# Sorting neighbour lists on the VectorE: exchanges and products in operations of at most 384 elements

## The chip, the cores and the metric

The kernel runs on one core of a Trainium2 chip. The core has five engines that work side by side, each with its own queue of instructions: PE (matmuls), DVE (elementwise work on vectors), ACT (activations and copies), POOL (GpSimd, which here issues the indirect DMAs), and SP (which issues the plain DMAs). The metric is the device time of one execution in microseconds. Several timed executions are made without the profiler, and one more with it; the profile is of that one.

## The reference

There are 16 graphs of 1024 nodes with 64 features each. Of every graph's adjacency matrix some edges are dropped by a rule on degrees. Then each node takes, for each feature, the quartiles of the values of its remaining neighbours, itself included, adds them with weights to its own value, and sends the sum through a two-layer perceptron.

```python
h = jnp.maximum(_layernorm(x, axis=-1), 0.0)
# inside the layer, with x = h:
adj_d = jnp.where(rem, 0.0, adj_)            # rem: the dropped edges, made symmetric
nd = adj_d > 0
vals = jnp.where(nd[..., None], x[:, None, :, :], jnp.inf)
s = jnp.sort(vals, axis=2)                   # the neighbours' values, sorted, per feature
nv = nd.sum(2)
for tau, w in zip((0.25, 0.5, 0.75), (0.25, 0.5, 0.25)):
    pos = tau * jnp.maximum(nv - 1, 0)
    lo, hi = jnp.floor(pos), jnp.ceil(pos)
    agg = agg + w * (v_lo + (pos - lo) * (v_hi - v_lo))   # v_lo, v_hi: s at lo and hi
out = x + agg
y = jax.nn.relu(out @ W1 + b1) @ W2 + b2
return x_in + y * mask
```

A node has few neighbours, so the kernel doesn't sort over 1024 values: it gathers the neighbours' rows and sorts short lists.

## The kernel before

Graphs ("batches" in the code) are prepared one by one: `load`, `drop`, `keep`, `order` and `collect` turn the adjacency matrix into lists of neighbour indices. `order` arranges the nodes of a graph by their number of neighbours, in eight tiles of 128 nodes: tile 0 has the longest lists, tile 7 the shortest. The tiles are put into four classes, by the number of slots that a list gets:

```python
CLASSES = (((0,), 13), ((1, 2, 3), 11), ((4, 5), 9), ((6, 7), 7))
```

Two graphs make a pair, and there are eight pairs. For each class of a pair there is one buffer `g` of shape [128 nodes, slots, tiles, 2 graphs, 64 features] in 32-bit floats. One slot of it, over all tiles of the class and both graphs, thus has 128 elements in a partition for tile 0, 384 for tiles 1 to 3, and 256 for tiles 4 and 5 and for tiles 6 and 7. The buffer is filled by indirect DMAs from POOL, one for each slot of each tile and graph (`gather`, line 1250): 128 rows of 256 bytes each. There are 1008 of them in all. The longest 32 lists of a graph are kept aside and sorted eight graphs at a time, in a group buffer `gg` of 24 slots with 128 elements each.

`sort` (line 1271) works on one buffer after the other. Its plan (`PLANS`) is a list of steps. A step takes `n` slots from place `a` with stride `da`, and `n` slots from `b` with stride `db`. With `f` at zero or more it is a full exchange: the minima (or maxima) of the two go to free slots from `f` on (line 1288), and the other of the two goes in place, over `a` or `b` (line 1289). With `f` below zero only one of the two is wanted (line 1285). After the steps the slots that hold the wanted ranks are multiplied by their weights (line 1296, the products, `taken` slots at a time), and 128x128 identity matmuls on PE add them up in PSUM (line 1298). The DVE does all steps and products; `n` is up to 3 for tile 0 and the group, up to 2 in the other classes, and the products of classes 9 and 7 take three slots at a time.

Two things go along with each step. The generator yields an estimated cost, and `weave` uses it to interleave the sort of one pair with the preparation of the next and with the issue of gathers. And `let_go` adds up these costs: from 0.8 on it puts a small memset of a tile `pause` (line 1268) behind the instruction that it is given.

The order in which the instructions were written is not the order in which the engines run them. `arrange` takes the whole program, works out which instruction depends on which, and plays it through with an estimated cost for each (for a DVE instruction (elements + 66) / 0.96 ns, and 115 ns more until a dependent one on the DVE can follow). Whenever an engine is free, it takes the earliest written instruction that is ready. The result is laid down as the fixed order of each engine. A `pause` stays tied to the instruction that it was put behind, and a run of matmuls (`settle`) is kept together.

Of the kernel before, what the change touches and what calls it, by code (L numbers as in the profile page):

```python
# [40 lines left out]
OP = mybir.AluOpType  # L41
# [4 lines left out]
C = 64  # L46
# [40 lines left out]
BIG = 3.0e38  # L87

SPREAD = 160


FIRST = CAPS[0] - 1
# [656 lines left out]
def list_layer(  # L749
# [14 lines left out]
    nc = tc.nc  # L764
# [10 lines left out]
    def settle(run):  # L775

        runs.append([ins.ins.name for ins in run])
        for ins, then in zip(run, run[1:]):
            tc.add_manual_dep(
                then.ins, ins.ins.name,  # L780
                mybir.DependencyInfo(mybir.DependencyClass.NoSync, mybir.DependencyReason.DATA),
                reason="order of a run",
            )
            tc.add_to_no_dep_group(f"run{len(runs)}", ins.ins)
            tc.info.no_tile_sem_insts.add(ins.ins.name)
        if len(run) > 1:
            tc.declare_fence(run[-1].ins, group=f"run{len(runs)}")
# [30 lines left out]
    plus, minus, upper, full, octet, one = (kw[:, lo:hi] for lo, hi in zip(FP8_PARTS, FP8_PARTS[1:]))  # L818
# [410 lines left out]
    def issue(many=None):  # L1229

        while queue and (many is None or many > 0):
            ins = queue.popleft()()
            if ins is None:
                continue
            turn[0] += 1
            many = None if many is None else many - 1
# [28 lines left out]
    def let_go(held, ins):  # L1265
        if held < 0.8:
            return held
        tails[nc.vector.memset(pause, 0.0).ins.name] = ins.ins.name  # L1268
        return 0.0

    def sort(lines, plan, first, coef, acc):

        size = lines.shape[2]
        held = 0.0

        def at(first, step, n):
            stop = first + step * (n - 1) + (1 if step >= 0 else -1)
            return lines[:, first:stop if stop >= 0 else None:step or 1]

        _, _, steps, ends, taken = plan  # L1280
        for n, a, da, b, db, f, df, back, what in steps:
            pa, pb = at(a, da, n), at(b, db, n)
            cost = 0.16 + n * size / 960
            if f < 0:
                ins = nc.vector.tensor_tensor(pa if back else pb, pa, pb, OP.min if what == "min" else OP.max)
            else:
                one, other = (OP.min, OP.max) if what == "<" else (OP.max, OP.min)
                nc.vector.tensor_tensor(at(f, df, n), pa, pb, one)  # L1288
                ins = nc.vector.tensor_tensor(pa if back else pb, pa, pb, other)  # L1289
                cost *= 2  # L1290
            yield cost
            held = let_go(held + cost, ins)
        for n in taken:
            now, ends = ends[:n], ends[n:]
            v = at(now[0], now[1] - now[0] if n > 1 else 0, n).rearrange("p s (k c) -> p s k c", c=C)
            ins = nc.vector.tensor_tensor(v, v, coef(first, n)[:, :, :, None].to_broadcast(list(v.shape)), OP.mult)
            settle([
                nc.tensor.matmul(  # L1298
                    acc, ident32, lines[:, s], start=False, stop=(s == now[-1] and not ends), skip_group_check=True
                )  # L1300
                for s in now
            ])
            first += n
            cost = 0.16 + n * size / 960
            held = let_go(held + cost, ins)
            yield cost
# [22 lines left out]
    def aggregate(m, o):  # L1329
# [4 lines left out]
        for half in (0, 1) if last else (1, 0):  # L1334
# [21 lines left out]
            for tiles, slots in parts:  # L1356
                lo, n = tiles[0], len(tiles)
                g = gathered.pop((m, tiles))
                plan = PLANS[slots]
                yield from sort(  # L1360
                    g.rearrange("p s n h c -> p s (n h c)"), plan, window(tiles, slots)[0],
                    lambda s, many: coef[:, s:s + many, lo:lo + n].rearrange("p s n h -> p s (n h)"),
                    acc[:, lo - 4 * half:lo - 4 * half + n],
                )
# [100 lines left out]
    def aggregate_group(grp):  # L1465
        n = GROUP // 4
        gg = groups.pop(grp)
        to, xg = gathered.pop(("group", grp))
        coef = wk.tile([P, TOP, n], F32, name="gcoef", bufs=1)
        weights(coef, group_num[grp][:, :, 1], n, TOP)  # L1470
        yield 1.0
        acc = psum.tile([P, n, C], F32, name="gacc", tag="agg", bufs=2)
        nc.tensor.matmul(acc, ident32, gg[:, CAP - 1], start=True, stop=False, skip_group_check=True)
        yield from sort(
            gg.rearrange("p s k c -> p s (k c)"), PLANS[CAP], window((0,), CAP)[0],
            lambda s, many: coef[:, s:s + many], acc.rearrange("p k c -> p (k c)"),
        )
        o = wk.tile([P, n * C], F32, name="go", tag="lows", bufs=1)
        nc.scalar.copy(o, acc.rearrange("p k c -> p (k c)"))
        yield 0.0  # L1480
        tp = psum.tile([P, P], F32, name="ot", tag="misc")
        nc.tensor.transpose(tp, o, ident32)
        ot = wk.tile([P, P], F32, name="got", tag="h1", bufs=1)
        nc.scalar.copy(ot, tp)
        yield 0.0
        h1 = wk.tile([P, n, P], F32, name="gh1", tag="highs", bufs=1)
        for k in range(n):
            hp = psum.tile([P, P], F32, name="hp", tag="misc")
            nc.tensor.matmul(hp, w1[k * C:(k + 1) * C], ot[k * C:(k + 1) * C], start=True, stop=True)
            nc.scalar.activation(h1[:, k], hp, AF.Relu, bias=b1c)  # L1490
            yield 0.0
        output(h1.rearrange("p k r -> p (k r)"), n, group_num.pop(grp)[:, :, 0], xg)
        gathered["out", grp] = to, xg
# [9 lines left out]
    def weave(main, total, side, side_total):  # L1503
# [3 lines left out]
        for cost in main:  # L1507
            done += cost / total
            issue(max(0, int(done * SPREAD) - turn[0]))
            while side is not None and spent / side_total < done:  # L1510
# [261 lines left out]
```

## Time and profile before

| what | us |
|---|---|
| timed runs, median of 3 (lowest to highest) | 2607.62 (2595.87 to 2612.22) |
| profiled execution, its own time | 1581.97 |
| span in the profile, first to last instruction | 1580.2 |
| POOL busy | 1137.8 |
| DVE busy | 1191.0 |
| PE busy | 1071.0 |
| ACT busy | 917.2 |
| gathers of line 1250, 1008 of them | 1089.7 |
| exchanges of lines 1288 and 1289, classes' buffers, 408 each | 280.7 and 281.4 |

The profile is of one execution. A line of the table of groups reads: line of the code, engine, operation, what is written and read, how many; then the busy time in us and the mean duration of one in ns; then the idle time of the engine just ahead of these instructions, and what ended it. A line of the waits reads: who waited, for what, us in total, number of times, the longest in us. A line of a timeline reads: start in us, duration in us, engine, line, operation, what is written and read. A line of the stretches reads: from and to in us, the length, and then the busy time of PE, PE's weight loads, DVE, ACT and POOL with their numbers of instructions.

### The profile page before, as it was taken

To read this page: it belongs to the slowest core of one execution; us is meant where nothing else is said; L and a number is where in the kernel's file an instruction comes from. 1 tells how busy PE (TensorE), PEld (TensorE's weight loads), DVE (VectorE), ACT (ScalarE), POOL (GpSimd) and SP (SyncE) were. 2 spreads that over 40 slices of the span, in tenths; PEclk is the share of its full clock that TensorE was granted. 3 is DMA by queue.
4 is the path that set the end of the run, shared out by engine and by line. 5 is a ranking of instruction groups with operands and counts; after the bars stand their busy time and mean duration, and the time that the engine had idled before them with its cause. 6 is when DMAs were issued, how large, how long until landed. Compare 5 with 4: busy or idle time off the path is not lost.

```text
span 1580.2 us, 25600 instructions
## 1 busy us (share of the span) xinstructions
PE 1071.0 (68%) x8385; PEld 664.2 (42%) x8385; DVE 1191.0 (75%) x3723; ACT 917.2 (58%) x2496; POOL 1137.8 (72%) x1051
## 2 busy tenths in 40 slices
PE   6777867889887887888569845588758822602235
PEld 3444544555554555455245534354535412301122
DVE  5615489865997789868884899977988897697660
ACT  6998886987958695978367841766825300200001
POOL 3277776777777777777777777777777777777730
PEclk9989979899998999899679976899888955855568
DMA  6453432442523252325122422222311211211100
GB/s 208 118 159 93 116 110 62 113 116 64 149 69 112 53 149 58 111 59 143 50 71 73 118 78 45 73 84 56 86 28 26 46 31 26 55 24 23 22 11 18
DMA packets 128481, 122.71 MB, mean 78 GB/s; under 512 B 94514, under 2 KB 95026, under 8 KB 128338
## 3 DMA queue, kind: packets, MB, share of 16 engines
q1 hardware_dynamic: 94994, 86.77, 19.4%
q0 software_dynamic: 33344, 34.21, 9.7%
q8 instruction: 68, 1.11, 0.3%
q14 instruction: 75, 0.61, 0.1%
HBM read 110.10 MB, written 9.07 MB: 75 GB/s over the span
## 4 chain that ended last, share of the span: by engine, by line
POOL 32%; ACT 20%; PE 14%; issue 14%; DVE 12%; DMA 6%; DVEq 0%; POOLq 0%; SPq 0%; ACTq 0%
POOL g L1250 31%; PE codeP L1072 5%; DMA g<-gtab,idx 4%; ACT dist L978 4%; ACT sg L891 3%; DVE g L1288 3%; ACT ne L911 3%; DVE g L1289 2%; ACT kept L1001 2%; ACT waste L1170 2%; ACT waste L1165 1%; ACT xt L1178 1%; PE acc L1298 1%; PE rk L968 1%; DMA xt<-in_x_dram 1%
## 5 line engine op out<-in xcount | busy, mean ns | idle before, releaser
L1250 POOL DMA_INDIRECT g<-gtab,idx x1008 | 1089.7, 1081 | 361.3 <-issue 288.0
L1288 DVE TENSOR_TENSOR g<-g 128x512 f32<-128x512 f32 (+3 forms) x408 | 280.7, 701 | 40.9 <-DMA g<-gtab,idx 25.9
L1289 DVE TENSOR_TENSOR g<-g 128x512 f32<-128x512 f32 (+3 forms) x408 | 281.4, 702 | 11.1 <-DMA gg<-g 8.4
L1298 PE MATMUL acc<-g,kf 128*128 128x256 f32 (+2 forms) x448 | 143.4, 461 | 176.5 <-DVE pause L1268 105.2
L1072 PE MATMUL codeP<-pack,perm 128*128 128x332 bf16 x1024 | 185.3, 323 | 21.4 <-DVE perm L1047 18.4
L978 ACT ACTIVATE dist<-rk,bias 128x512 f16<-128x512 f32 x256 | 168.4, 698 | 27.8 <-DVE bias L953 10.7
L1298 PEld LDWEIGHTS acc<-g,kf 128*128 128x128 f32 x448 | 89.5, 231 | 204.1 <-DVE pause L1268 111.4
L968 PE MATMUL rk<-kb,cnt 128*128 128x512 bf16 x256 | 113.2, 442 | 74.5 <-ACT dist L978 68.2
L1001 ACT ACTIVATE kept<-kp 128x512 fp8e4<-128x512 f32 x248 | 149.2, 617 | 14.0 <-PE kp L996 11.9
L898 PE MATMUL tp<-kb,sg 128*128 128x128 bf16 x1024 | 106.8, 243 | 69.3 <-ACT sg L891 52.6
L911 ACT ACTIVATE ne<-tp 128x512 fp8e4<-128x512 f32 x248 | 138.2, 608 | 19.4 <-PE tp L904 10.7
L973 PEld LDWEIGHTS <-ne 128*128 128x128 fp8e4 x1024 | 90.2, 109 | 133.1 <-issue 110.8
L1072 PEld LDWEIGHTS <-perm 128*128 128x128 bf16 x1024 | 93.9, 101 | 85.3 <-DVE perm L1047 43.9
L891 ACT ACTIVATE sg<-at 128x1024 bf16<-128x1024 f32 x121 | 126.6, 1076 | 2.4 <-DMA at<-in_adj_dram 2.3
L898 PEld LDWEIGHTS <-sg 128*128 128x128 bf16 x1024 | 81.2, 110 | 91.1 <-ACT sg L891 61.1
L973 PE MATMUL rk<-kw,ne 128*128 128x128 fp8e5 x1024 | 118.0, 243 | 0.0
L979 DVE TENSOR_SCALAR rem<-dist,half 128x1024 bf16<-128x1024 f16 x128 | 64.7, 506 | 61.7 <-ACT dist L978 60.7
L996 PE MATMUL kp<-kw,rem 128*128 128x128 fp8e5 x1024 | 99.7, 219 | 0.0
L991 PE MATMUL kp<-ne,kw 128*128 128x512 fp8e4 x256 | 98.5, 385 | 0.1
L992 PE MATMUL kp<-rem,kw 128*128 128x512 bf16 x256 | 97.6, 382 | 0.0
L1077 ACT CAST st<-codeP 128x4 bf16<-128x4 f32 x128 | 21.1, 165 | 119.6 <-PE codeP L1072 119.5
L1373 DVE TENSOR_SCALAR at_p<-iota,node 128x512 bf16<-128x512 f16 x256 | 82.8, 370 | 6.8 <-PE low L1397 6.7
(178 smaller groups left out, 2051.1 us busy)
## 6 DMA issues: line engine op xcount, KB each, us to landing
at<-in_adj_dram SPq DMA_DIRECT2D x122, 512.0 KB
g<-gtab,idx POOLq DMA_INDIRECT x1008
xt<-in_x_dram SPq DMA_DIRECT2D x16, 256.0 KB
y<-in_x_dram SPq DMA_DIRECT2D x16, 256.0 KB
gtab<-xt SPq DMA_DIRECT2D x16, 256.0 KB
out_dram<-y SPq DMA_DIRECT2D x16, 256.0 KB
spare<-in_adj_dram SPq DMA_DIRECT2D x6, 512.0 KB
gg<-g SPq DMA_DIRECT2D x32, 48.0 KB
```

Source lines behind the costliest of these rows:

```text
L891: nc.scalar.activation(sg, at, AF.Sign)
L898: run.append(nc.tensor.matmul(tp[:, s], sg[:, m * P:(m + 1) * P], ident16, start=(s == 0), stop=(s == 3 and t // 4 != n), skip_group_check ...
L911: nc.scalar.activation(to, tp, AF.Relu, saturate=False)
L968: run = [nc.tensor.matmul(rk, cnt[:, ts], blocks[:, 4 * n:4 * n + 4, None].to_broadcast([P, 4, P]), start=True, stop=False, skip_group_che ...
L973: run.append(nc.tensor.matmul(rk[:, s * P:(s + 1) * P], ne[:, 4 * n + s, ts], upper, start=False, stop=(s == 3), skip_group_check=True,))
L978: nc.scalar.activation(dist[:, n * HALF:(n + 1) * HALF], rk, AF.Abs, bias=bias[:, t:t + 1])
L1001: nc.scalar.activation(kept[:, 4 * n:4 * n + 4], kp, AF.Relu, saturate=False)
L1072: run.append(nc.tensor.matmul(flat, perm[:, t, k * P:(k + 1) * P], pack[:, t], start=False, stop=(t == NT - 1), skip_group_check=True,))
L1250: return nc.gpsimd.indirect_dma_start(out=gathered[m, tiles][:, slot, k - lo, h], out_offset=None, in_=tables[2 * m + h][0], in_offset=bas ...
L1288: nc.vector.tensor_tensor(at(f, df, n), pa, pb, one)
L1289: ins = nc.vector.tensor_tensor(pa if back else pb, pa, pb, other)
L1298: nc.tensor.matmul(acc, ident32, lines[:, s], start=False, stop=(s == now[-1] and not ends), skip_group_check=True)
```

## The change

Every step and every product is cut along its slots into parts of at most 384 elements a partition. With `size` elements in a slot, `most` slots go into one part. A full exchange is done part by part: both halves of the first part, then both halves of the next. The estimated cost of a step stays what it was for the whole step, and `let_go` is still called once a step, with the last instruction of the last part. The matmuls behind the products are not changed.

```diff
+PART = 384
...
         _, _, steps, ends, taken = plan
+        most = max(1, PART // size)
+
+        def parts(n):
+            return [(k, min(most, n - k)) for k in range(0, n, most)]
+
         for n, a, da, b, db, f, df, back, what in steps:
-            pa, pb = at(a, da, n), at(b, db, n)
-            cost = 0.16 + n * size / 960
-            if f < 0:
-                ins = nc.vector.tensor_tensor(pa if back else pb, pa, pb, OP.min if what == "min" else OP.max)
-            else:
-                one, other = (OP.min, OP.max) if what == "<" else (OP.max, OP.min)
-                nc.vector.tensor_tensor(at(f, df, n), pa, pb, one)
-                ins = nc.vector.tensor_tensor(pa if back else pb, pa, pb, other)
-                cost *= 2
+            for k, many in parts(n):
+                pa, pb = at(a + k * da, da, many), at(b + k * db, db, many)
+                if f < 0:
+                    ins = nc.vector.tensor_tensor(pa if back else pb, pa, pb, OP.min if what == "min" else OP.max)
+                else:
+                    one, other = (OP.min, OP.max) if what == "<" else (OP.max, OP.min)
+                    nc.vector.tensor_tensor(at(f + k * df, df, many), pa, pb, one)
+                    ins = nc.vector.tensor_tensor(pa if back else pb, pa, pb, other)
+            cost = (0.16 + n * size / 960) * (1 if f < 0 else 2)
             yield cost
             held = let_go(held + cost, ins)
         for n in taken:
             now, ends = ends[:n], ends[n:]
-            v = at(now[0], now[1] - now[0] if n > 1 else 0, n).rearrange("p s (k c) -> p s k c", c=C)
-            ins = nc.vector.tensor_tensor(v, v, coef(first, n)[:, :, :, None].to_broadcast(list(v.shape)), OP.mult)
+            for k, many in parts(n):
+                some = now[k:k + many]
+                v = at(some[0], some[1] - some[0] if many > 1 else 0, many).rearrange("p s (k c) -> p s k c", c=C)
+                ins = nc.vector.tensor_tensor(
+                    v, v, coef(first + k, many)[:, :, :, None].to_broadcast(list(v.shape)), OP.mult
+                )
```

## The prediction

> **What bounds the kernel now.** I read the table of engines and the chain that ended last first, then the waits of POOL, then the forms of the DVE's sort instructions, and at last the timelines of POOL and DVE side by side.
>
> ```profile
> PE 1071.0 (68%) x8385; PEld 664.2 (42%) x8385; DVE 1191.0 (75%) x3723; ACT 917.2 (58%) x2496; POOL 1137.8 (72%) x1051
> POOL 32%; ACT 20%; PE 14%; issue 14%; DVE 12%; DMA 6%; DVEq 0%; POOLq 0%; SPq 0%; ACTq 0%
> L1250 POOL DMA_INDIRECT g<-gtab,idx x1008 | 1089.7, 1081 | 361.3 <-issue 288.0
> ...
> POOL g L1250 <- issue: 288.0, 945, 0.3
> POOL g L1250 <- DVE idx L1116: 55.0, 3, 46.0
> ```
>
> The gathers of line 1250 run from 68 us to 1517 us of the 1580 us span. In 945 of 1008 cases the gap ahead of one is the 0.30 us that POOL needs between two, with nothing waited for; only the first three real waits, 55 us together, are for data. POOL's stream of gathers sets the end of the profiled execution, and 65 us of tail follow it. The DVE stands close behind:
>
> ```profile
> 680.00:720.00 40.00, 37.12 (x216) 20.14 (x215) 28.22 (x108) 26.47 (x97) 30.86 (x31) 1.00 0.28 66
> 1240.00:1280.00 40.00, 18.55 (x91) 9.97 (x90) 40.00 (x109) 7.78 (x19) 31.16 (x30) 0.77 0.25 51
> ```
>
> Third pair of numbers: the DVE is busy for 28 us of 40 in one stretch and for all 40 in another. Its work is the sort:
>
> ```profile
> L1289 DVE TENSOR_TENSOR g<-g 128x768 f32<-128x768 f32 x128 | 121.5, 949 | 0.6
> L1288 DVE TENSOR_TENSOR g<-g 128x512 f32<-128x512 f32 x136 | 92.6, 685 | 15.1 <-DMA g<-gtab,idx 11.5 <-issue 3.2
> L1296 DVE TENSOR_TENSOR g<-g,coef 128x768 f32<-128x768 f32 x64 | 59.2, 950 | 0.1
> L1289 DVE TENSOR_TENSOR g<-g 128x384 f32<-128x384 f32 x88 | 47.9, 550 | 8.6 <-DMA gg<-g 8.4
> L1289 DVE TENSOR_TENSOR g<-g 128x256 f32<-128x256 f32 x56 | 23.5, 419 | 0.3
> ```
>
> And the two engines touch each other. A gather takes 944 ns when undisturbed (940 the shortest, 952 the median), but 1081 on average:
>
> ```profile
> 1273.63 1.25 POOL L1250 DMA_INDIRECT g<-gtab,idx  x1 [0.30 <-issue]
> ...
> 1255.57 1.90 POOL L1250 DMA_INDIRECT g<-gtab,idx  x1 [0.30 <-issue]
> ...
> 1256.85 0.95 DVE L1288 TENSOR_TENSOR g<-g 128x768 f32<-128x768 f32 x1
> ```
>
> Set against the DVE's timeline, a long gather ends some 890 ns after the end of the DVE instruction with two SBUF inputs, or of the fast one-input kind, that was running when it came. Over the 1008 gathers the time beyond 944 ns sums to 142 us; 245 of them stood behind a sort instruction of 512 or 768 elements, for 93 us.
>
> **One thing the profile leaves open.** The profiled execution took 1581.97 us (span 1580.2), the timed runs 2607.62: 1.65 times as much. No view shows the other 1025 us. One sum comes near: if gathers and DVE never ran together, the time would be the DVE's 1191 us, plus 1042 indirect DMAs at 0.944 + 0.30 us, 1296 us, plus the stretches where neither works, 68 - 37 = 31 us ahead of the first gather and 65 - 16 = 49 us after the last one: 2567 us, 40 short of the median. So I take it that in the timed runs a gather that meets a busy DVE isn't let in at the next instruction's start, as it is in the trace, but only when the DVE pauses for something. That is an inference from one sum.
>
> [...] from start to start, 768 elements take 877 ns, 512 take 610, 384 take 477 and 256 take 343, each the elements at 0.96 GHz plus 76 or 77 ns.
>
> **The change, part by part.**
> Only classes of 11, 9 and 7 slots split: a slot has 384 elements there for tiles 1 to 3 and 256 for the two pairs of tiles. Tile 0 and the group sort (128 a slot, at most three slots in an operation) stay as they are.
> - Exchanges. Per pair of batches, class 11 has 35 instructions and gets 67 (its 32 of 768 elements become 64 of 384), class 9 goes from 27 to 47 and class 7 from 17 to 31 (34 of 512 become 68 of 256). That is 66 more, 528 over eight pairs. The trace's counts agree: 128 + 128 of 768, 136 + 136 of 512.
> - Products. Class 11: four of 768 become eight of 384. Classes 9 and 7: four of 768 become twelve of 256. That is 12 more a pair, 96 in all.
> - Cost on the DVE. 288 instructions of 768 become two of 384: 954 - 877 = 77 ns each, 22.2 us. 272 of 512 become two of 256: 686 - 610 = 76 ns, 20.7 us. 32 of 768 become three of 256: 1029 - 877 = 152 ns, 4.9 us. Sum 47.7 us for 624 instructions.
> - What is won back. An exchange's second half waits for the first, and the next step for both; where nothing else is ready, such a step costs 109 ns more (725 rather than 610 in the tail, from 1519 us on). There are 144 of these short stalls behind the sorts' instructions, 15.6 us. The planner starts another ready instruction in a stall, and the other part is one. Between 0 and 15 us; I take 8.
> - The pauses. A step's cost for `let_go` and for the weave is computed as before, so the 578 memsets of line 1268 and the order of issue stay; a pause is now behind the last part. The time between two grows from 1754 to 1908 ns for a step of 768.
> - Waits. No wait for another engine, no DMA and no queue is added. Each part may wait for its own gathers instead of for all of the step (27 us of DVE waiting for landings in all, little of it here). The matmuls of line 1298 stay one run behind the last product. The planner orders all engines anew, with 69 ns more for each extra instruction; I cost a changed order at nothing, with 10 us either way for luck.
> - POOL. If a gather is let in at the next start, 118 of the 245 gathers that stood behind a long instruction would have come in at the new start in its middle, and save half of it: 46.5 us. If it isn't, nothing.
>
> Sum on the DVE: 48 - 8 = 40 us. By the sum above, where DVE and gathers alternate, each microsecond of DVE work is one of the whole: 2607.6 + 40 = 2648 us.
>
> **The rivals.**
> - *Gathers come in earlier.* This is the profiled execution's own behaviour: POOL sets the end, and the DVE has room (1191 of 1580 us). The stream shortens by 46.5 us, and the last sort after the last gather, with 18 to 42 more instructions, gets up to 3 us longer: -43, so 2565 us. For it: every long gather in the trace. Against it: this behaviour gives 1582 us, not 2607, so something else must add the 1025. It decides as soon as half a sort instruction saved over more than about 86 gathers (40 us) outweighs the DVE's longer work.
> - *Hidden.* The 1025 us are a share that neither engine's sort touches, or gain and cost meet: 2607, between 2585 and 2633. For it: the DVE's 25% of idle time. Against it: DVE stretches at 40 of 40.
> - *Starved further.* If a gather in the timed runs comes in only where the DVE stalls or pauses, fewer stalls and longer stretches between pauses (1908 for 1754, 9%) cost more than the instructions themselves: 9% of the 1025 us would be 92, so 2700. Against it: only a third of the stretches are of this kind.
> - That the change doesn't split is excluded: the counts follow from the plans.
>
> **How the numbers follow.** DVE work added: 0.52, at 2648 (2625 to 2685, with the won-back part from 0 to 15 and 10 for the order). Gathers earlier: 0.25, at 2565 (2555 to 2590). Hidden: 0.17. Starved further: 0.06. One per cent, 26 us, is about what a measurement can tell from no change. Faster by more: 0.25 (nearly all of the second case); within: 0.22 (most of hidden, the low edge of the first); slower: 0.53. Both signs hold much of the chance, so the range goes from the low end of one to the high end of the other, 2555 to 2690; the likeliest case alone has 2625 to 2685.
>
> **What would show it.** In the changed profile: no form of 128x768 or 128x512 at lines of `sort` that now are exchanges; exchanges of classes 11, 9 and 7 as 165 instructions a pair with their products, not 87; DVE busy near 1191 + 40 to 48; the same 578 pauses. Gathers should average less than 1081 ns, nearer 1035, and the profiled span may even shrink by up to 43 us; then only the timed runs tell the first case from the second. The prediction is wrong if the timed runs follow the profiled span, or if the extra 1025 us shrink with the length of a DVE instruction.

## The result

| | kernel before | changed kernel |
|---|---|---|
| timed runs, median of 4 each, us | 2609.92 (2595.87 to 2621.63) | 2689.51 (2675.43 to 2692.77) |
| ratio, changed to before | | 1.0281, 95% interval 1.0241 to 1.0320 |
| span of the changed kernel's profile, us | | 2691.0 |

The change costs 80 us by the medians (73 by the ratio); the forecast was 40. The sign and the range of the prediction hold, and most of its reasons don't. The range holds by luck: the median lies 0.5 us inside its upper end of 2690, and outside the 2625 to 2685 of the likeliest case.

One thing has to be known to read any number below: the same program runs on some chips in about 1581 us and on others in about 2610 us, in timed and profiled executions alike, and by its time the profile that the prediction was made from belongs to the first sort, while the timed runs belong to the second. The runs below were made on three chips of the first sort and two of the second, each used on one occasion, so whether the difference is lasting isn't known. On the first sort the change is not a loss: it makes the kernel 2.2% faster.

The page of the changed kernel, from the second sort of chip: the table of engines, their busy share in 40 slices (tenths), the chain that ended last, and three groups: the gathers, the exchanges' second halves, and a step of the preparation on ACT.

```profile
PE 1163.4 (43%) x8370; PEld 704.7 (26%) x8385; DVE 1220.7 (45%) x4347; ACT 924.6 (34%) x2496; POOL 1017.1 (38%) x1051
...
DVE  5112067134416460456239241693832381191893
ACT  7164355225515360425333270523632040001001
POOL 1714332562354237262530627115074617406000
...
DVE 4%; issue 1%; PE 1%; DMA 0%; ACT 0%; POOL 0%; POOLq 0%; DVEq 0%
...
L1251 POOL DMA_INDIRECT g<-gtab,idx x1008 | 972.2, 964 | 1361.8 <-PE acc L1308 679.9
L1295 DVE TENSOR_TENSOR g<-g 128x256 f32<-128x256 f32 (+1 forms) x672 | 312.1, 486 | 34.8 <-remote 16.6
L979 ACT ACTIVATE dist<-rk,bias 128x512 f16<-128x512 f32 x256 | 170.1, 698 | 305.6 <-remote 210.4
```

No engine is busy for half of the span. POOL's digits and DVE's take turns: where POOL has 7, DVE has 0 to 3. The gathers take 964 ns, hardly more than the 944 of an undisturbed one, so nothing starves them; POOL instead stands 1362 us still ahead of them. The chain is broken off after 6% of the span and says nothing here. In place of it, six lines of the waits:

```profile
POOL g L1251 <- PE acc L1308: 679.9, 11, 110.7
DVE rem L980 <- ACT dist L979: 366.4, 68, 48.5
POOL g L1251 <- issue: 322.6, 967, 28.2
...
POOL g L1251 <- DVE idx L1117: 255.2, 5, 77.2
...
ACT ne L912 <- remote: 226.6, 28, 21.1
ACT dist L979 <- remote: 210.4, 25, 47.6
```

"Remote" is a wait that no instruction in the trace accounts for at the time it ends. What it is can be seen in the timeline (start, duration, engine, line):

```profile
244.42 0.15 PEld L905 LDWEIGHTS <-kb 128*128 128x128 bf16 x1
244.53 0.31 PE L905 MATMUL tp<-kb 128*128 128x128 bf16 x1
...
246.20 0.94 POOL L1251 DMA_INDIRECT g<-gtab,idx  x1 [0.31 <-issue]
247.45 0.95 POOL L1251 DMA_INDIRECT g<-gtab,idx  x1 [0.30 <-issue]
248.70 0.94 POOL L1251 DMA_INDIRECT g<-gtab,idx  x1 [0.30 <-issue]
249.95 0.95 POOL L1251 DMA_INDIRECT g<-gtab,idx  x1 [0.31 <-issue]
250.45 0.60 ACT L912 ACTIVATE ne<-tp 128x512 fp8e4<-128x512 f32 x1 [5.86 <-remote]
```

PE is done with `tp` at 244.84 us. ACT, which waits for it, starts at 250.45. By the trace it waits for a semaphore that PE's instructions increment (1292 of them in this profile). The increment that precedes its start is recorded at 250.43, 5.6 us after the matmul. Meanwhile POOL issues one gather every 1.25 us. I call an unbroken row of indirect DMAs (all 1042 of them, the 1008 gathers included, with less than 0.5 us between two) a streak. There are 25, for 1315 of the 2691 us. Taking the time from an instruction's end to the next recorded increment of its engine, many increments that PE, ACT and DVE make inside streaks are late: half of PE's by 1.7 us or more, a tenth by 21 us or more, some of DVE's by up to 95 us. Of those made outside, half come within 15 ns. About a tenth of DVE's and ACT's increments have no record of their own in this profile (DVE's 3489 have 3131), so a single lateness can be overstated; the waits above don't depend on it. During a streak the other engines got little done here; when it ended, because POOL itself needed something (`acc` of PE for 679.9 us and `idx` of DVE for 255.2 in the waits above), they went on:

```profile
720.00:800.00 80.00, 13.90 (x45) 7.88 (x46) 8.27 (x29) 5.89 (x16) 52.36 (x55) 0.50 0.12 23
800.00:880.00 80.00, 43.76 (x410) 30.43 (x408) 47.26 (x160) 44.55 (x92) 31.66 (x32) 0.76 0.32 85
```

These are two stretches of 80 us with the busy times of PE, weight loads, DVE, ACT, POOL. In the first one, 69 us of which are streak, DVE works 8.3 us; in the second, with 41 us of streak, 47.3.

The exchanges themselves came out as planned:

```profile
L1295 DVE TENSOR_TENSOR g<-g 128x384 f32<-128x384 f32 x344 | 184.1, 551 | 21.5 <-issue 7.3 <-DMA gg<-g 5.2 <-remote 3.7
L1294 DVE TENSOR_TENSOR g<-g 128x384 f32<-128x384 f32 x344 | 182.5, 551 | 1.5 <-DVE g L1294 0.7
L1295 DVE TENSOR_TENSOR g<-g 128x256 f32<-128x256 f32 x328 | 129.7, 417 | 13.3 <-remote 12.8
L1294 DVE TENSOR_TENSOR g<-g 128x256 f32<-128x256 f32 x328 | 129.4, 419 | 0.4
```

No exchange of 768 or 512 is left, and DVE has 4347 instructions for 3723, the 624 more that were counted.

### The profile page after: what moved, and what is told of

Its sections match the earlier page's. It is cut to its first block, busy times and chain, and to the rows that moved or that the text cites. A ratio compares the mean times of both kernels' runs of the same rounds, so it can differ in the third digit from the quotient of the medians.

```text
span 2691.0 us, 26238 instructions
## 1 busy us (share of the span) xinstructions
PE 1163.4 (43%) x8370; PEld 704.7 (26%) x8385; DVE 1220.7 (45%) x4347; ACT 924.6 (34%) x2496; POOL 1017.1 (38%) x1051
## 5 line engine op out<-in xcount | busy, mean ns | idle before, releaser
L1251 POOL DMA_INDIRECT g<-gtab,idx x1008 | 972.2, 964 | 1361.8 <-PE acc L1308 679.9
L1295 DVE TENSOR_TENSOR g<-g 128x256 f32<-128x256 f32 (+1 forms) x672 | 312.1, 486 | 34.8 <-remote 16.6
L1294 DVE TENSOR_TENSOR g<-g 128x256 f32<-128x256 f32 (+1 forms) x672 | 310.2, 486 | 1.9 <-DVE g L1294 0.7
L899 PE MATMUL tp<-kb,sg 128*128 128x128 bf16 x1024 | 117.3, 258 | 331.8 <-ACT dist L979 166.1
L969 PE MATMUL rk<-kb,cnt 128*128 128x512 bf16 x256 | 123.5, 482 | 310.7 <-ACT dist L979 191.5
L1073 PE MATMUL codeP<-pack,perm 128*128 128x332 bf16 x1024 | 195.4, 335 | 21.4 <-DVE perm L1048 21.0
L974 PEld LDWEIGHTS <-ne 128*128 128x128 fp8e4 x1024 | 99.7, 118 | 366.9 <-issue 348.8
L1442 DVE TENSOR_TENSOR yp<-yp,mask 128x256 f32<-128x256 f32 x32 | 13.8, 430 | 324.2 <-remote 229.1
L974 PE MATMUL rk<-kw,ne 128*128 128x128 fp8e5 x1024 | 132.7, 260 | 1.8 <-issue 1.8
L1088 DVE MAX8 keys<-codeP 128x8 f32<-128x128 f32 x128 | 37.8, 297 | 206.0 <-ACT own L1083 101.4
L1420 PE MATMUL hp<-highs,w 128*128 128x512 f32 x64 | 43.4, 765 | 200.3 <-ACT highs L1414 102.9
```

The costliest lines, as they stand in the source:

```text
L899: run.append(nc.tensor.matmul(tp[:, s], sg[:, m * P:(m + 1) * P], ident16, start=(s == 0), stop=(s == 3 and t // 4 != n), skip_group_check ...
L969: run = [nc.tensor.matmul(rk, cnt[:, ts], blocks[:, 4 * n:4 * n + 4, None].to_broadcast([P, 4, P]), start=True, stop=False, skip_group_che ...
L974: run.append(nc.tensor.matmul(rk[:, s * P:(s + 1) * P], ne[:, 4 * n + s, ts], upper, start=False, stop=(s == 3), skip_group_check=True,))
L1073: run.append(nc.tensor.matmul(flat, perm[:, t, k * P:(k + 1) * P], pack[:, t], start=False, stop=(t == NT - 1), skip_group_check=True,))
L1251: return nc.gpsimd.indirect_dma_start(out=gathered[m, tiles][:, slot, k - lo, h], out_offset=None, in_=tables[2 * m + h][0], in_offset=bas ...
L1294: nc.vector.tensor_tensor(at(f + k * df, df, many), pa, pb, one)
```

## The experiments

All kernels do the whole computation. The first theory was the prediction's (theory A: a microsecond of DVE work is a microsecond of the whole), its rivals that the new order of issue costs the time (theory B), that the mere number of instructions does, and that the gathers come in earlier (theory C). Beside the medians stand those of the kernel before on the same chip.

### The kernel before once more, and the cut without a new order

The first run changes nothing.

> The kernel before, unchanged, to get a profile of it that can be set beside the changed kernel's. The changed kernel's profile (span 2691.0 us) shows the DVE nearly idle while POOL issues a streak of gathers, and increments of semaphores by PE, ACT and DVE that are recorded up to 95 us late in such a streak. Theory A (work added one for one): this profile shows the same alternation, a span of about 2608 us, gathers at their undisturbed 944 ns, and outside the gathers about 48 us less DVE work than after. Rival (the two profiles differ because of the change): a span of 1580 us again, without late increments.

Measured: 1581.73 us, not 2610. This and the next three kernels ran on a chip of the first sort, while the numbers expected of them, but for the last rival here, were for the second and aren't put to the test by them. That rival, by which the change itself makes the two profiles differ, expected just this time; the changed kernel on a chip of the first sort and the kernel before on one of the second, both below, rule it out. Its table of engines and its group of gathers:

```profile
PE 1073.5 (68%) x8385; PEld 665.3 (42%) x8385; DVE 1192.3 (75%) x3723; ACT 917.6 (58%) x2496; POOL 1138.8 (72%) x1051
...
L1250 POOL DMA_INDIRECT g<-gtab,idx x1008 | 1090.9, 1082 | 360.3 <-issue 288.4
```

DVE is busy for 1192 us here, and in a profile of the same kernel from the second sort, shown further below, for 1186. PE is busy 91 us longer there, 1165 for 1074, at a mean granted clock of 0.70 for 0.85; whether that clock is cause or consequence of the waiting isn't shown, but 91 us don't make up 1037. Nearly all of the 1025 us that the prediction left open are therefore not work but waiting, and they belong to the chip at that time, not to the kernel. Among the waits of PE, ACT and DVE in this profile not one is "remote". Inside streaks, 98 of 100 of PE's increments come within 24 ns, and 99 of 100 of ACT's and DVE's within 11.

In the second kernel the parts of an instruction are one unit for `arrange`, at the price of the uncut instruction, and follow directly on each other. The order of PE, ACT, POOL and SP is then that of the kernel before, instruction by instruction; only DVE has 624 more.

```diff
-def arrange(tc, runs, tails=()):
+def arrange(tc, runs, tails=(), joined=()):
...
+        if ins.name in joined:
+            at, part = found[joined[ins.name]], Step(ins, 0)
+            at.reads += part.reads
+            at.writes += part.writes
+            at.more.append(ins)
+            at.elements += part.elements
+            at.busy = (at.elements + 66) / 0.96
+            found[ins.name] = at
+            continue
...
-        line = [i for s in steps for i in (s.ins, *(next(alike) for _ in s.tail))]
+        line = [i for s in steps for i in (s.ins, *s.more, *(next(alike) for _ in s.tail))]
```

> All 624 cuts, but the planner sees the parts of one instruction as one step at its old price, so the order of every engine is that of the kernel before, with the parts of an instruction back to back. Theory A (cost of the added DVE instructions alone): the whole loss stays, 2680 to 2695 us, if all of it is per-instruction cost; 2640 to 2660 us if it is 77 ns for each of the 624, 48 us. Theory B (the planner's new order makes the loss): at most 2625 us. In between, the split between the two can be read off.

Measured: 1550.16 us against 1580.79, ratio 0.9803 (0.9783 to 0.9824). The cut alone is a gain of 31 us on this chip.

```profile
PE 1069.3 (69%) x8385; PEld 663.1 (43%) x8385; DVE 1228.6 (79%) x4347; ACT 915.5 (59%) x2496; POOL 1101.3 (71%) x1051
...
L1261 POOL DMA_INDIRECT g<-gtab,idx x1008 | 1053.7, 1045 | 365.7 <-issue 287.7
```

DVE works 36 us longer, and the gathers 37 us less (1082 to 1045 ns each). The last gather ends at 1485.5 us instead of 1517.3. POOL's stream sets the end here, so its saving is the one that counts. As the order on the other engines is the old one, the gain is the cut's and not that of a new order.

### Smaller parts, and instructions that hold nothing

```diff
-PART = 384
+PART = 128
```

> Parts of at most 128 elements in place of 384: tile 0 and the group sort are cut as well, 1410 instructions more than before where the change has 624. Theory A at 77 ns each: 109 us, about 2718 us. Theory A at what the change cost (80 us for 624, 128 ns each): 180 us, about 2790 us. Theory B (order): no relation to the count, anywhere from 2610 to 2700 us.

Measured: 1533.79 us, ratio 0.9708 (0.9677 to 0.9740). There are 1410 further instructions instead of 624 and DVE is busy for 1266.1 us, 74 more than before; still the whole gets 47 us shorter.

```profile
L1251 POOL DMA_INDIRECT g<-gtab,idx x1008 | 1039.3, 1031 | 366.4 <-issue 285.2
```

Next, the instructions stay uncut, and 624 memsets of one element go behind those that the change cuts, one for each part more, in the order of before.

```diff
+    def extra(ins, n, size):
+        for _ in range(-(-n // max(1, 384 // size)) - 1):
+            more = nc.vector.memset(pause, 0.0).ins.name
+            tails[more] = ins.ins.name
+            unpriced.add(more)
+        return ins
```

> No instruction is cut. Instead a memset of one element is put behind each instruction that the change cuts, one for each further part, 624 in all, with the order of everything else as before. They read nothing, nobody waits for them, and in the profiles such a memset runs beside the instruction ahead of it. Theory A (the loss is DVE time in the sorts): within 10 us of before, 2600 to 2620 us, or up to 35 us more if a memset holds back the next instruction by 60 ns. Rival (the number of DVE instructions or of their semaphore increments counts, whatever they do): 2660 us or more.

Measured: 1579.16 us, ratio 0.9995 (0.9982 to 1.0007): no difference. The gathers keep their length (1077 ns). So further instructions alone, or more pauses, don't help; of the explanations named, the length of what a gather has to sit out is left.

### The changed kernel on this sort of chip, and half of the cut

The first of these is the changed kernel itself.

> The changed kernel, unchanged, beside the kernel before on one chip. In the first four experiments the kernel before took 1580.8 us, no increment of a semaphore was late, and the cut with the old order took 1550 us; in the recorded comparison it took 2610 us and the changed kernel 2690 us, with late increments in the changed kernel's profile. If the kernel before again takes about 1581 us here, theory C (a gather waits for the DVE instruction [...], and shorter instructions let it in sooner) expects 1540 to 1555 us, gathers 32 to 45 us shorter in sum; theory A (DVE work is added one for one) expects 1620 to 1630 us. If the kernel before takes about 2610 us, both expect 2680 to 2695 us again.

Measured: 1548.55 us against 1582.65, ratio 0.9782 (0.9756 to 0.9809), so 34 us less.

```profile
PE 1075.3 (69%) x8385; PEld 664.7 (43%) x8385; DVE 1225.7 (79%) x4347; ACT 915.7 (59%) x2496; POOL 1102.3 (71%) x1051
...
L1251 POOL DMA_INDIRECT g<-gtab,idx x1008 | 1055.8, 1047 | 364.7 <-issue 286.4
```

This is the rival "gathers come in earlier". The prediction gave it 43 us, 46.5 won by the gathers less 3 for a longer end; what they take beyond 944 ns fell from 139.3 us in the first run to 104.2 here, by 35.1. The planner's new order makes no difference that these runs can tell: this interval and that of the cut with the order kept overlap.

The other kernel keeps the order and cuts only the classes of 9 and 7 slots (512 to 256), 336 of the 624.

```diff
-        most = max(1, PART // size)
+        most = 1 if size == 256 else 3
```

> Only the classes of 9 and 7 slots are cut (slots of 256 elements): 336 of the 624 further instructions, in the order of the kernel before. The class of 11 slots keeps its instructions of 768 elements. Without late increments, theory C: the gathers that stood behind instructions of 512 (28 us beyond the undisturbed time in sum, 12 us to be won) and behind the two products of 768 a class (a third of 13 us) gain, about 15 us, so 1562 to 1572 us where before takes 1581. A rival (the gain of the order-kept cut comes from anything that grows with the count of instructions): 336/624 of its 31 us, 1564 us; the two are told apart by the gathers' sum, not by the time. With late increments, theory A: 336/624 of the 80 us, about 2653 us where before takes 2610.

Measured: 1566.76 us, ratio 0.9902 (0.9885 to 0.9920), 16 us less, with the gathers' time beyond 944 ns at 123.0 us, also 16 less. Half of the cut, half of the gain; and in each of the kernels so far the span follows the gathers: against the first run it changes by -1 to -49 us, and the gathers' sum by -5 to -52, within some 4 us of it each time.

### On the other sort of chip: without pauses, and in parts of 128

The first kernel is that of before without its 578 pauses, with their price left in the planner, so that all orders stay.

```diff
-        tails[nc.vector.memset(pause, 0.0).ins.name] = ins.ins.name
+        owed.add(ins.ins.name)
...
+        found[ins.name].busy += (1 + 66) / 0.96 if ins.name in owed else 0
```

> The kernel before without its 578 memsets of one element behind the sorts' instructions; the planner still counts their price, so the order of everything else is as before. Where the kernel before takes about 1581 us, theory C as the prediction had it (a gather is let in at the start of the next DVE instruction, whatever it is): no change, 1576 to 1588 us, and the gathers' time beyond 944 ns stays at 139 us in sum, give or take 8. Rival (a gather gets in only where a pause stands): over 1600 us and over 160 us in sum. Where the kernel before takes about 2610 us, theory A: no change within 15 us, since a pause costs the DVE next to nothing.

Measured: 2595.68 us against 2609.58, ratio 0.9939 (0.9913 to 0.9966). The pauses cost 14 us here, 24 ns each, and do no good: without them a gather takes 994 ns, with them 992. A kernel in which gathers came in where DVE pauses would have been hurt by losing 578 pauses; so the prediction's inference on the 1025 us, and with it the mechanism of "starved further", falls for this sort of chip.

The second is the cut in parts of 128 with the order of before.

> Parts of at most 128 elements with the order of the kernel before: 1410 further DVE instructions. Where the kernel before takes about 1581 us, theory C: the same gain as with the planner's own order, a ratio of 0.967 to 0.975. Rival (part of that gain was the new order): 0.978 or above. Where it takes about 2610 us, theory A at 77 ns: 2719 us; at the 128 ns that the change showed: 2790 us; if the changed kernel's loss was its order: 2640 us or less.

Measured: 2718.67 us, ratio 1.0432 (1.0373 to 1.0492), 109 us more for 1410 instructions: 77 ns for each, as theory A expected. Parts of 128 made the kernel 47 us faster on a chip of the first sort (there in the planner's own order) and make it 109 us slower here.

### The cut with the order kept, on a chip with late increments

The kernel of the second experiment and the kernel before, once more.

> The 624 cuts of the change with the order of the kernel before, as in the second experiment, to be had on a chip where increments come late. There (before about 2610 us) the 1410 cuts with the old order cost 109.1 us, which is 77 ns each, as theory A says. Theory A expects 624 x 77 ns = 48 us here, 2653 to 2663 us; the other 32 of the change's 80 us are then its order. Rival (the loss isn't in proportion to the count): 2680 us or more, or 2630 us or less. Where the kernel before takes about 1581 us, 1545 to 1555 us again.

> The kernel before, unchanged, for its profile on a chip where increments come late. Expected there: a span of 2590 to 2620 us, streaks of gathers of about 1340 us in sum, increments of PE, ACT and DVE late inside the streaks, and about 350 us of DVE work inside them, as without the pauses (the seventh experiment); the changed kernel has 256 us inside. On a chip where they are on time: 1581 us.

Measured: 2686.33 us against 2620.88, ratio 1.0250 (1.0182 to 1.0317), and 2618.46 for the kernel before. The cut alone, with nothing moved on any other engine, costs 65 us here (48 to 83). That is most of the 80 of the result, and the two intervals overlap: whether the new order adds anything can't be said. The 48 us of theory A lie at the edge of the interval, and 2686.33 lies in the range of its rival. With 65 us for 624 instructions and 109 for 1410, the loss doesn't look proportional to their number.

The profile of the kernel before from this sort of chip, table of engines, the gathers and one wait:

```profile
PE 1164.6 (45%) x8371; PEld 705.1 (27%) x8385; DVE 1185.7 (45%) x3723; ACT 928.7 (35%) x2496; POOL 1045.2 (40%) x1051
...
L1250 POOL DMA_INDIRECT g<-gtab,idx x1008 | 1000.0, 992 | 1268.0 <-PE acc L1298 413.3
...
ACT ne L911 <- remote: 194.4, 23, 25.3
```

It has the late increments too. With streaks as defined above, the five profiles from such chips split as follows (us; "inside" and "outside" are of the streaks; a span is its streaks plus DVE busy outside plus DVE idle outside):

| kernel | span | streaks | DVE busy outside | DVE idle outside | DVE busy inside | sort instructions begun inside |
|---|---|---|---|---|---|---|
| before | 2616.8 | 1342.9 | 847.7 | 426.2 | 338.0 | 244 of 1198 |
| before without pauses | 2595.7 | 1344.6 | 829.9 | 421.2 | 350.4 | 272 of 1198 |
| cut, order kept | 2685.1 | 1321.6 | 943.3 | 420.2 | 280.8 | 288 of 1822 |
| changed kernel | 2691.0 | 1314.8 | 964.5 | 411.7 | 256.3 | 257 of 1822 |
| parts of 128, order kept | 2715.6 | 1317.3 | 983.7 | 414.6 | 283.8 | 355 of 2608 |

For the changed kernel against that of before the span grows by 74: DVE outside the streaks +117, its idle time there -14, the streaks -28. The 117 have two parts. DVE has 35 us more work in all, and 82 us of its work no longer get done inside the streaks. The last column suggests why: from the kernel before to the parts of 128 the sort instructions more than double (1198 to 2608) and those begun inside streaks only grow from 244 to 355, so with shorter instructions the streaks let through less work (338.0 us of DVE inside them before, 283.8 with the parts). In the changed kernel 257 sort instructions begin inside streaks where 244 did, but one of them takes 497 ns on average instead of 746. Sort work makes up 58 of the 82 us (177 to 119 us inside); the other 24 are other work of DVE, which the reading leaves unexplained. No run here varies that alone, so it is argued from five profiles, not shown. The -28 is the gathers' gain, 992 to 964 ns; it exists here too, but pays for only a quarter of the loss.

### What lets a gather in

Two kernels on a chip with timely increments: the kernel before without pauses again, and the cut in parts of 128 without pauses (the planner's own order).

> The kernel before without its 578 pauses and with its order, as in the seventh experiment, which fell on a chip with late increments (2595.7 against 2609.6 us). On a chip where they are on time (before about 1581 us), theory C expects that a gather needs no pause to get in: 1576 to 1588 us, its time beyond 944 ns 139 us in sum, give or take 8. Rival (a gather gets in only at a pause): over 1600 us and over 160 us in sum. With late increments: 10 to 20 us less than before again.

> Parts of at most 128 elements as in the third experiment, with its order, and without the pauses: the fastest version that the runs so far point to where increments are on time. Theory C: 1525 to 1540 us there, where before takes 1581 and the third experiment 1534, since gathers get in without pauses. With late increments: 2690 to 2720 us, the DVE's added work less some 14 us for the pauses.

Measured: 1619.06 us (1611.57 to 1649.69) for the first, ratio 1.0220 (1.0173 to 1.0267), and 1754.60 us (1738.19 to 1788.15) for the second, ratio 1.1052 (1.0986 to 1.1117). In the first, the gathers take 173.5 us beyond 944 ns, 34 more than in the kernel before, the span is 33 us longer, and one gather waited 22.3 us behind 34 DVE instructions, most of them of 768 and 384 elements. That is the rival's forecast (over 1600 us, over 160 in sum), and theory C as the prediction had it is refuted. If a gather were let in at the next start of any DVE instruction, the second would have taken the expected 1525 to 1540 us. Its profile is of the longest of its four executions, 1788.15 us; even the shortest is 155 us above the kernel before. Its POOL timeline:

```profile
1534.01 2.78 POOL L1252 DMA_INDIRECT g<-gtab,idx  x1 [0.30 <-issue]
1537.10 51.28 POOL L1252 DMA_INDIRECT g<-gtab,idx  x1 [0.31 <-issue]
1588.68 0.95 POOL L1252 DMA_INDIRECT g<-gtab,idx  x1 [0.30 <-issue]
```

And DVE's over the same time, cut to its first and last lines:

```profile
1537.37 0.68 DVE L1294 TENSOR_TENSOR gg<-gg 128x128 f32<-128x128 f32 x3
1537.97 0.48 DVE L1293 TENSOR_TENSOR gg<-gg 128x128 f32<-128x128 f32 x2
1538.38 0.48 DVE L1294 TENSOR_TENSOR gg<-gg 128x128 f32<-128x128 f32 x2
...
1583.85 3.51 DVE L1303 TENSOR_TENSOR gg<-gg,gcoef 128x128 f32<-128x128 f32 x17
1587.28 0.28 DVE L1294 TENSOR_TENSOR g<-g 128x128 f32<-128x128 f32 x1
1587.59 0.29 DVE L1293 TENSOR_TENSOR g<-g 128x128 f32<-128x128 f32 x1
1587.92 0.29 DVE L1294 TENSOR_TENSOR g<-g 128x128 f32<-128x128 f32 x1
```

The gather that begins at 1537.10 us takes 51.28 us. In that time DVE begins 253 instructions with two SBUF inputs, one every 202 ns, with no gap between any two of them until the last four: the instruction of 1587.28 is over at 1587.56, and the next begins at 1587.59. The gather ends 0.8 us after that, at 1588.38. The six longest waits of this kernel are 51, 44, 24, 16, 12 and 9 us; in the kernel before, with pauses, none is over 2.6.

So the rule of the prediction ("let in at the next instruction's start") was too kind, and the example that it was read from shows how. The gather of 1.90 us ran from 1255.57 to 1257.47 us. These are DVE's lines over that time, ahead of the one of 1256.85 that the prediction has:

```profile
1255.71 0.95 DVE L1289 TENSOR_TENSOR g<-g 128x768 f32<-128x768 f32 x1
1256.59 0.34 DVE L1373 TENSOR_SCALAR at_p<-iota,node 128x512 bf16<-128x512 f16 x1
1256.61 0.06 DVE L1268 MEMSET pause<- 128x1 f32 x1
```

The gather sat behind the first of these, which ends at 1256.66, and ended 0.81 us after it; the exchange of 1256.85 began only then. Of the 438 gathers of 1 us or more in that profile, 402 end 0.81 to 0.82 us after the end of a DVE instruction, which is 0.89 us after the start of the next one where two overlap. Which instructions hold one up shows there too: of the gathers that find a single DVE instruction running 0.1 us after their own start, 360 of 429 take 1 us or more when it is one of `sort`, with two SBUF inputs, 59 of 104 when it is a one-input TENSOR_SCALAR from f16 to bf16 (lines 979, 1047 and 1373), and 3 of 78 when it is a MAX8 or a MATCH_REPLACE8. By the mark of 0.82 us I counted, for gathers of 1 us or more, the starts of a sort instruction that follows directly on another one, with neither pause nor gap: the first such start after the gather came, and the later ones.

| kernel, all with timely increments | first start: let in, passed over | later starts: let in, passed over |
|---|---|---|
| before | 124, 1 | 0, 1 |
| changed kernel | 190, 11 | 3, 2 |
| parts of 128 | 187, 22 | 7, 16 |
| before without pauses | 148, 19 | 0, 48 |
| parts of 128 without pauses | 150, 84 | 1, 972 |

Without pauses a gather that isn't let in at the first start is, with one exception, not let in at a later one either, until the row of sort instructions ends. A gap between two sort instructions let a waiting gather in each time, 97 of 97 in these five profiles. The six longest waits of parts of 128 without pauses all end 0.82 us after a sort instruction behind which DVE had a gap or ran an instruction of another kind. What decides at the first start isn't found; none of the gathers let in there had come less than 0.1 us before it.

A pause ends such a row, and one follows the step with which 0.8 us of sort, by the estimated cost, are reached. With pauses, parts of 128 give 0.9708, without them 1.1052: that the pauses keep such waits from happening is shown for these kernels. In the last kernel, too, the span went with the gathers: 206 us longer than in the first run, for 205 in the gathers' sum.

## Why the prediction was right, and where it was not

**POOL's stream sets the end, DVE close behind.** Right for the execution in that profile, and borne out on such chips: in all kernels there the span went with the gathers, to within some 4 us. It didn't hold for the timed runs that were to be forecast. Three of its readings are a little off: the gathers' time beyond 944 ns is 138 us by the group's own 1089.7, not 142; 63 us follow the last gather, not 65; and a long gather ends 0.82 us, not 0.89, after the end of the instruction that it sat behind.

**The open 1025 us.** The step failed. The gathers are not what is held up: with late increments they take 992 ns, less than the 1082 with timely ones. PE, ACT and DVE wait for increments while gathers stream: half of PE's came 1.7 us late or more in the streaks of the changed kernel, and ACT's `ne` alone waited 194.4 us for "remote" in the kernel before. The sum that came to 2567 had the alternation right in the main and its details wrong, and came near by luck: 338 us of DVE work do lie beside the gathers, where the sum had none, and DVE is idle for 426 us outside the streaks, where it had 80; the two errors, 338 and 346 us, nearly cancel. The prediction's own sign of being wrong came true: on either sort of chip the timed runs follow the span of the profile taken there (2689.5 and 2691.0 us for the changed kernel, 1548.6 and 1547.5).

**Counts and cost on DVE.** The counts are right, 624 instructions, and the cost nearly. The sort's own busy time grew by 43 us (737.2 to 780.3, late increments) and by 43 (739.3 to 781.9, timely ones), within the 40 to 48 named; DVE's busy time as a whole, for which they were named, by 35 and 33.

**Won-back stalls, 8 us.** Not separable. DVE's idle time outside the streaks fell by 14 us, with the order kept by 6.

**Pauses, waits, order.** There are 578 pauses as said. The order's 10 us either way was neither refuted nor confirmed: 80 us by the medians, 73 by the ratio (63 to 84) with it, against 65 (48 to 83) without.

**POOL's part.** 46.5 us if gathers come in at the next start, and nothing otherwise. With timely increments 35 us were saved, three quarters. With late ones 28 us were saved, and DVE's longer time outside the streaks cost more than that.

**The sum.** Its last step, that each microsecond of DVE work is one of the whole, is the term that was mis-sized: 40 us forecast, 80 measured. The added instructions (35 us of busy time) are in it; the 82 us of work that move out of the streaks are what it lacked, and 42 us of shorter streaks and less idle time stand against them. So the forecast's sign rests on a fact that is right in the main, that DVE's time and that of the gathers add up in those runs (of DVE's 1185.7 us before, 847.7 lay outside the streaks); the cause that it gave for it was wrong.

**The rivals.** "Gathers come in earlier" is what happens on a chip with timely increments, 34 us instead of 43. "Starved further" named a time near the measured one (2700), by a mechanism that the run without pauses on a chip with late increments rules out there. On chips with timely increments pauses do matter (1.0220 without them), which is where the prediction did not look for it. "Hidden" occurred on neither.

None of these kernels is faster than the one before on both sorts of chip. With timely increments the parts of 128 are best (0.9708); with late ones the kernel before without its pauses is (0.9939), which loses 2.2% on the others.

## What to carry to other kernels

When the profiled execution and the timed runs differ by more than their spread, look for what differs between the executions before reasoning from the profile; a sum that comes out near the missing time is no explanation. Cutting DVE instructions that held up GpSimd's gathers cost here 76 to 77 ns of DVE for each further piece, from start to start, and shortened the gathers' waits, by 35 us for 624 pieces with timely increments. It paid where the stream of gathers set the end (ratio 0.9782) and not where DVE's time added to the whole (1.0281). Shorter pieces didn't replace a pause: without pauses a gather waited 51.28 us behind an unbroken run of 128 elements each, as one waited 22.3 us behind a run of mostly 384 and 768.

## What was not expected of the hardware

In the profile of the changed kernel from the second sort of chip, half of PE's increments of its semaphore, made while POOL issued gathers at 1.25 us each, were recorded 1.7 us late or more and some of DVE's up to 95 us; in the profile that the prediction was made from, half of PE's came within 14 ns. The changed kernel took 2690 us on one sort and 1549 on the other. What sets these chips apart is open. And a gather waited 51.28 us behind a row of DVE instructions of 128 elements, one every 202 ns, and came in when the row had its first gap, of 34 ns.
